# Two batches of a conditioned residual kernel as one product during its weight-loading phase, with base and rank terms put into PSUM banks

## The chip, the cores and the metric

One core of one Trainium2 chip runs the whole program. The metric is the device time of one execution in microseconds (us), the median of several runs. TensorE (PE in the profile) multiplies matrices, VectorE (DVE) and ScalarE (ACT) do elementwise work, GpSimd (POOL) and SyncE (SP) here mostly issue DMAs; ScalarE issues the stores of the output. SBUF holds tiles of 128 partitions[...].

## What is computed

For 8 batches b, with x[b] of 1024 x 512, cond[b] of 512, and weights:

```python
ae = layernorm(cond, ln_g, ln_b)
h  = gelu(ae @ w1 + b1)
xw = h @ w2 + b2                      # 8 x 8192
x_a, x_b = split(xw), each reshaped to (8, 512, 8)
layer = base + einsum('bdr,bkr->bdk', x_a, x_b)
x = x + (x + x @ layer)               # L0, its own residual and the outer one
ys = cond / sqrt(512)
d  = rsqrt((ys*ys) @ (weight*weight) + 1e-8)
x = x + ((x * ys) @ weight) * d       # L1
```

Both layers are linear in x, so the kernel makes one 512 x 512 matrix P[b] per batch and computes out[b] = x[b] @ P[b]:

- n[b] = I + diag(ys[b]) weight diag(d[b]), the matrix of L1 with its residual;
- P[b] = (2 I + base + x_a x_b^T) n[b] = (2 I + base) n[b] + x_a (n[b]^T x_b)^T. The first part is called q[b], the second is the rank term (rank 8).

f32 accuracy comes from splitting every operand into a high part in the format fp32r and the rest, and from three matmuls (high x high, high x rest, rest x high) for one.

## The kernel before

**Order.** `mm` (line 45) pins the order of all matmuls. Until `InOrder.on = False` (line 805) the instructions of VectorE, ScalarE and SyncE stand in the order of the source, too (`InOrder`, line 62 is the line that they all carry in the profile). After that, until the last two batches, a scheduler of the framework places those of VectorE, ScalarE and the DMAs, and lists in `after` (`at`, line 957) say behind which tile of the main part each step is emitted. Buffers are handed out by pools: a tile waits until whoever held its memory is through. `big` has nine buffers of 1 MB for weights, x, q and others; `acc` has four PSUM banks for products, `misc` and `xps` two each during the fill, replaced by `po` (four) in the main part.

**Fill.** While 16 groups of w2 (1 MB each, `w2_group`, line 389; each asks for its load on SyncE's queue at the place where its four matmuls stand) come in, TensorE makes q[0] to q[3], each alone: q[0] with `first_base`, the others with the class `Fill`, whose `units` (line 534) each do 3 matmuls: 4 chunks of the contraction by 4 row blocks by 3, 48 a batch. `n_half` makes two of four chunks of n[b] with VectorE, `round_right` makes its high part (ScalarE) and the rest (VectorE). The left matrix 2 I + base^T lies in `bh`/`bl`, split from `b_raw`, where the transposed base was loaded. Its four sums for the two-batch product (`left_sum`, line 368) are made at the very end of the fill.

**Rank term.** `rank_t` makes the right factor t, `with_bias`/`split`/`stack` the left factor a. `stack` brings them into rows of 4 batches (group g = 0 for batches 0 to 3, 1 for 4 to 7), keeps them in SBUF (`st_t`, `st_a`, pool `sp`), and stores them in DRAM (`kept_t`, `kept_a`). `load_rank(b)` (line 505) fetches 8 pieces of 64 KB for batch b on GpSimd's queue into the tiles `fa`, `ft` of `npool`; `rank_term(b)` (line 514) multiplies them into four `acc` banks and adds these to q[b] with VectorE. For batch 0 this is done straight from SBUF (`rank_first`, line 497, with the masked tile of `mask_t`), and base, loaded a second time untransposed (`b_nat`), is added to q[0] with 2 I on its diagonal. `split_p` splits P into `ph` (ScalarE) and `pl` (VectorE).

**Main part.** 48 tiles (batches 0 to 5, 8 tiles of 128 rows each): `main(b, t)` does 12 matmuls into a `po` bank, ScalarE copies it to `o` and issues its store. `load_x` and `split_x` prepare x four tiles ahead. Behind tiles stand `load_rank` 1 (tile 0), 2 (0), 3 (2), `rank_term` 1, 2, 3 (tiles 2, 5, 8), and from tile 11 on the class `Pair`, which makes q of two batches from seven products (Strassen's scheme) of 12 matmuls, for batches 4, 5 and 6, 7. `Pair.unit` (line 611) does half a product, 6 matmuls. Batches 6 and 7 are multiplied by seven products, too (`Seven`), at the end.

Of the kernel before, what the change touches and what calls it, by code (L numbers as in the profile page):

```python
# [30 lines left out]
def cond_resid_kernel(ctx: ExitStack, tc: tile.TileContext, small, cond, condrows, consts,  # L31
# [100 lines left out]
    def right_tiles(name):  # L132

        h = npool.tile([P, 2, D], F32R, tag="nh", name=f"nh_{name}")
        l = npool.tile([P, 2, D], F32R, tag="nl", name=f"nl_{name}")
        return h, l
# [196 lines left out]
    def n_half(b, j):  # L333

        n = npool.tile([P, 2, D], F32, tag="n", name=f"n_{b}_{j}", bufs=4)
        for kk in range(2):
            k = 2 * j + kk
            ve.scalar_tensor_tensor(n[:, kk, :], w_sb[:, k, :], ysT[:, k, b:b + 1],
                                           d_all[b], ALU.mult, ALU.mult)
            blk = n[:, kk, k * P:(k + 1) * P]  # L340
            ve.tensor_add(blk, blk, ident)
# [26 lines left out]
    def left_sum(i):  # L368
# [20 lines left out]
    def w2_group():  # L389
# [8 lines left out]
        if len(todo) == 6:  # L398
# [36 lines left out]
    def rank_t():  # L435
# [111 lines left out]
    class Pair:  # L547
# [63 lines left out]
        def unit(self):  # L611
# [55 lines left out]
    def split_x(b, j, part=None):  # L667
# [5 lines left out]
        if part != 0:  # L673
            ve.tensor_sub(xs[b, j][:, 1], t, xs[b, j][:, 0].bitcast(F32))
# [20 lines left out]
    class Fill:  # L695


        def __init__(self):
            self.bases = [Base(b) for b in (1, 2, 3)]
            self.ns, self.rests = {}, {}  # L700

        def units(self, count):
            for _ in range(count):
                if self.bases[0].at == 4 * KC:
                    self.bases.pop(0)
                self.bases[0].units(1)

        def make_n(self, b, j):
# [383 lines left out]
```

## Time and profile before

| | |
|---|---|
| median of 3 runs | 302.5 us (301.93 to 302.55) |
| the profiled execution | 302.08 us, its span 300.3 us |
| TensorE's clock | 1.00 over the span |
| first tile of the main part starts | 80.52 us |
| end of the main part's tiles | 254.59 us |
| DMA | 62.14 MB, mean 207 GB/s; 410 to 425 GB/s from 10 to 50 us |

Times within the execution are us from the start of the span. In the chain of waits a row is start, duration, what, and how many instructions; in the timeline of an engine start, duration, engine, line, operation, tiles out<-in, count and in brackets the idle time before it with what ended it; in the table of windows the stretch, its length, busy time (and count) of PE, PEld, DVE, ACT and POOL, the granted clock, the DMA share and GB/s; in the groups busy time and mean ns, then idle time before them. A tile's name has no buffer numbers: `w<-in_w` are the groups of w2 (and w1 where its tile is `w_sb`).

### The profile page before, as it was taken

Reading aid. Unit: us, or ns where it says so; the run is one execution under the profiler, and the core shown is the slowest. Engines: PE = TensorE matmul, PEld = TensorE weight load, DVE = VectorE, ACT = ScalarE, POOL = GpSimd, SP = SyncE. Lnnn points to the kernel's source line nnn. Section 1 sums busy time; section 2 is a strip of 40 time slices with the busy share of each in tenths; the row PEclk is TensorE's granted clock in tenths of the full one; section 3 lists DMA queues with packets and bytes.
Section 4 is the critical chain, followed back from the end, with each engine's and each line's share of the span. In section 5 each row is a group of like instructions: output and inputs, shape, how many; then the busy total and the mean of one; then the engine's idle time right before and its main releaser. Section 6 shows DMA issues by size and latency. Waiting matters only on the chain.

```text
span 300.3 us, 4005 instructions
## 1 busy us (share of the span) xinstructions
PE 293.4 (98%) x1501; PEld 227.1 (76%) x1501; DVE 211.0 (70%) x312; ACT 154.1 (51%) x226; POOL 34.8 (12%) x74
## 2 busy tenths in 40 slices
PE   7999999999999999999999999999999999999995
PEld 2655465466877778888887888888778888998995
DVE  4779840979569999935869994366562996479722
ACT  4757132256566673647634463656442663663630
POOL 0011000057004551000003600000000000000000
PEclk9999999999999999999999999999999999999999
DMA  7999999696619984605513841524516785131234
GB/s 210 410 428 419 405 424 419 219 326 183 197 70 305 306 288 126 239 35 210 204 43 97 230 164 46 201 55 192 210 70 210 244 267 227 38 140 49 93 140 142
DMA packets 19524, 62.14 MB, mean 207 GB/s; under 512 B 2720, under 2 KB 4000, under 8 KB 15152
## 3 DMA queue, kind: packets, MB, share of 16 engines
q1 hardware_dynamic: 6896, 39.57, 35.7%
q10 hardware_dynamic: 8832, 15.99, 14.2%
q0 software_dynamic: 3776, 6.31, 8.0%
q8 instruction: 12, 0.20, 0.3%
q14 instruction: 8, 0.07, 0.1%
HBM read 44.02 MB, written 17.84 MB: 206 GB/s over the span
## 4 chain that ended last, share of the span: by engine, by line
PE 84%; DVE 9%; ACT 3%; DMA 2%; issue 1%; SPq 0%; ACTq 0%
PE po L45 44%; PE pp L45 13%; PE pq L45 10%; PE sw L45 5%; PE px L45 4%; PE sz L45 2%; PE pg L45 2%; DVE n L62 2%; DMA b_raw<-in_baseT 2%; DVE sraw L62 1%; PE pr L45 1%; PE sv L45 1%; ACT o L62 1%; DVE sl L62 1%; ACT sh L62 1%
## 5 line engine op out<-in xcount | busy, mean ns | idle before, releaser
L45 PE MATMUL po<-ph,xs 128*128 128x512 f32 x384 | 123.8, 392 | 0.0
L45 PEld LDWEIGHTS po<-ph,xs 128*128 128x128 f32 x384 | 72.1, 188 | 16.8 <-issue 1.7
L45 PE MATMUL po<-pl,xs 128*128 128x512 f32 x192 | 74.8, 389 | 0.0
L62 ACT COPY o<-po 128x512 f32<-128x512 f32 x48 | 28.1, 586 | 52.8 <-PE po L45 52.8
L45 PEld LDWEIGHTS po<-pl,xs 128*128 128x128 f32 x192 | 36.1, 188 | 7.4
L62 DVE TENSOR_TENSOR xs<-x,xs 128x1024 fp32r<-128x1024 f32 x24 | 29.0, 1221 | 10.5 <-ACT xs L62 10.4
L62 ACT CAST xs<-x 128x1024 fp32r<-128x1024 f32 x24 | 24.9, 1052 | 3.7 <-DMA x<-in_x 1.9
L62 DVE TENSOR_TENSOR nl_p<-n,nh_p 128x1024 fp32r<-128x1024 f32 x14 | 17.1, 1222 | 12.3 <-ACT nh_p L62 12.2
L62 DVE TENSOR_TENSOR pl<-q,ph 128x1024 fp32r<-128x1024 f32 (+1 forms) x16 | 18.3, 1153 | 6.2 <-ACT ph L62 6.1
L62 DVE TENSOR_TENSOR q<-pr,q 128x512 f32<-128x512 f32 x32 | 20.1, 682 | 3.5 <-PE pr L45 3.5
L511 POOL DMA_DIRECT2D fa<-kept_a x28 | 13.7, 502 | 64.9 <-PE pr L45 64.8
L45 PE MATMUL pq<-nh,bh 128*128 128x512 f32 x48 | 19.8, 412 | 0.0
L45 PE MATMUL pq<-nl,bh 128*128 128x512 f32 x48 | 19.1, 398 | 0.1
L45 PE MATMUL pq<-nh,bl 128*128 128x512 f32 x48 | 19.0, 395 | 0.0
L62 DVE SCALAR_TENSOR_TENSOR n<-w_sb,ysT,d 128x512 f32<-128x512 f32 x24 | 17.7, 745 | 1.2 <-DMA d<-d_out 1.2
L62 ACT CAST nh_p<-n 128x1024 fp32r<-128x1024 f32 x14 | 14.8, 1054 | 6.3 <-PE pp L45 5.5
L62 ACT COPY o<-sw 128x512 f32<-128x512 f32 (+1 forms) x15 | 7.5, 500 | 19.2 <-PE sw L45 14.4
L62 ACT CAST ph<-q 128x1024 fp32r<-128x1024 f32 (+1 forms) x16 | 15.8, 1001 | 1.2 <-DVE q L62 0.8
L45 PE MATMUL px<-w,hT 128*32 128x512 f32 x128 | 16.0, 601 | 0.0
L62 ACT COPY q<-pp 128x512 f32<-128x512 f32 x20 | 11.7, 587 | 7.7 <-PE pp L45 7.7
L45 PEld LDWEIGHTS pq<-nh,bh 128*128 128x128 f32 x48 | 9.0, 188 | 8.4 <-issue 5.0
L511 POOL DMA_DIRECT2D ft<-kept_t x28 | 13.8, 509 | 5.2 <-DMA kept_t<-st_t 5.0
(185 smaller groups left out, 515.1 us busy)
## 6 DMA issues: line engine op xcount, KB each, us to landing
w<-in_w SPq DMA_DIRECT2D x16, 1024.0 KB, 10.5
x<-in_x SPq DMA_DIRECT2D x16, 1024.0 KB, 5.4
out<-o ACTq DMA_DIRECT2D x48, 256.0 KB, 3.2
out<-o ACTq DMA_DIRECT2D x6, 512.0 KB, 2.9
ft<-kept_t POOLq DMA_DIRECT2D x28, 64.0 KB, 3.4
fa<-kept_a POOLq DMA_DIRECT2D x28, 64.0 KB, 2.9
d<-d_out POOLq DMA_DIRECT2D x6, 256.0 KB, 5.2
w_sb<-in_weight SPq DMA_DIRECT2D x2, 512.0 KB, 5.3
```

Of the source, the lines that this page charges most:

```text
L45: tc.keep_in_program_order(nc.tensor.matmul(*args, **kw))
L62: return lambda *a, **kw: pin(f(*a, **kw)) if InOrder.on else f(*a, **kw)
L511: nc.gpsimd.dma_start(fold[name, b][32 * c:32 * c + 32, :], kept[name, g][32 * i:32 * i + 32, :])
```

## The change

- Batches 2 and 3 are made in the fill by `Pair(2)` instead of two bases; its last product (4) runs behind tiles 1 and 2 of the main part. The left sums are made in the middle of the fill (`left_raw`, `left_rest`). The four additions that end products 3 and 7 are held back (`hold`).
- `b_nat` is loaded two groups later. 2 I goes onto q[0]; `seed_first` puts q[0] + base into PSUM banks (`px` and `misc`), and the rank matmuls of batch 0 add onto them (32 rows, no mask). For batches 1 and 2, ScalarE copies q into the `acc` banks (`seed`), and the rank matmuls add onto that. `take` makes `ph` and `pl` of batches 0 to 2 out of the banks. Batch 3 stays as it was.
- The stacks of batches 4 to 7 are copied to `rows` and finished at the end of the fill (`late_rows`).
- `fa`, `ft` come from a new pool `folds`, opened after the fill's pools (`sp` among them) are closed. Loads and terms now: 1 (tiles 0, 3), 3 (1, 6), 2 (4, 9).
- The rest of the fourth x split of batch 0 is made by ScalarE (times -1) and an accumulating DMA; x (0, 1) is loaded in the fill. The identity is added to both blocks of a half of n in one instruction.

The diff, without the row of steps of the fill:

```diff
@@ -337,8 +337,8 @@
             k = 2 * j + kk
             ve.scalar_tensor_tensor(n[:, kk, :], w_sb[:, k, :], ysT[:, k, b:b + 1],
                                            d_all[b], ALU.mult, ALU.mult)
-            blk = n[:, kk, k * P:(k + 1) * P]
-            ve.tensor_add(blk, blk, ident)
+        blk = n.rearrange("p k (c i) -> p (k c) i", i=P)[:, 2 * j:2 * j + 6:5, :]
+        ve.tensor_add(blk, blk, ident.unsqueeze(1).to_broadcast([P, 2, P]))
         return n
     def round_right(n, name, wide=True):
@@ -365,7 +365,7 @@
     a11, a21 = b_raw[:, 0:2, 0:HD], b_raw[:, 0:2, HD:D]
     a12, a22 = b_raw[:, 2:4, 0:HD], b_raw[:, 2:4, HD:D]
-    def left_sum(i):
+    def left_raw(i):
         if i == 5:
             sraw["s"] = big_tile("sraw").rearrange("p k (u i) -> p k u i", u=2)
         s1, s2, s3, s4 = (sraw["s"][:, u] for u in range(4))
@@ -373,12 +373,14 @@
                        3: (s4, a12, s2, ve.tensor_sub), 7: (s3, a11, a21, ve.tensor_sub)}[i]
         op(s, x, y)
         h = cp.tile([P, 2, HD], F32R, name=f"sh_{i}")
+        se.copy(h, s)
+        sraw[i] = s, h
+    def left_rest(i):
+        s, h = sraw[i]
         l = cp.tile([P, 2, HD], F32R, name=f"sl_{i}")
-        se.copy(h, s)
         ve.tensor_sub(l, s, h.bitcast(F32))
         left[i] = h, l
-    b_nat = []
     px = [xps.tile([P, D], F32, name=f"px_{h}") for h in range(2)]
@@ -395,7 +397,7 @@
         if len(todo) == 8:
             sy.dma_start(crow, condrows)
             sy.dma_start(b2r, b2rows)
-        if len(todo) == 6:
+        if len(todo) == 4:
             b_nat.append(big_tile("b_nat"))
             sy.dma_start(b_nat[0], base)
         for j in range(4):
@@ -413,17 +415,27 @@
         ve.scalar_tensor_tensor(s, hi.bitcast(F32), neg_u, src, ALU.mult, ALU.add)
         return s
-    kept = {}
-    def stack(srcs, neg, name, g):
+    kept, late_rows = {}, []
+    def stack(srcs, neg, name, g, keep=None):
+        hi = None
         ps = misc.tile([P, D], F32, tag="misc", name=f"ps_{name}{g}")
         for i, src in enumerate(srcs):
             mm(ps, sel[:, g, :], src, start=(i == 0), stop=(i == len(srcs) - 1))
-        hi = work_tile()
-        se.copy(hi, ps)
+        if keep is None:
+            hi = work_tile()
+            se.copy(hi, ps)
+        else:
+            se.copy(keep, ps)
+            ps = keep
         def rest():
+            nonlocal hi
+            if keep is not None:
+                hi = work_tile()
+                se.copy(hi, ps)
             s = sp.tile([P, D], F32R, name=f"st_{name}{g}")
             ve.scalar_tensor_tensor(s, hi.bitcast(F32), neg, ps, ALU.mult, ALU.add)
             kept[name, g] = dram.tile([P, D], F32R, name=f"kept_{name}{g}")
@@ -463,24 +475,27 @@
         yield
         ve.tensor_sub(tl, t, th.bitcast(F32))
         yield
-        for g in range(2):
-            done = stack((th, tl), neg_t, "t", g)
-            yield
-            stt[g] = done()
-            yield
+        done = stack((th, tl), neg_t, "t", 0)
+        yield
+        stt[0] = done()
+        yield
+        late_rows.append(stack((th, tl), neg_t, "t", 1, rows[:, 3, :]))
+        yield
     def times_d(b, c):
         ve.tensor_mul(q[b][:, c, :], q[b][:, c, :], d_all[b])
-    def twice_i_plus_base():
-        for c in range(KC):
-            blk = b_nat[0][:, c, c * P:(c + 1) * P]
-            ve.scalar_tensor_tensor(blk, ident, 2.0, blk, ALU.mult, ALU.add)
-    def add_base(b):
-        for c in range(KC):
-            ve.tensor_add(q[b][:, c, :], q[b][:, c, :], b_nat[0][:, c, :])
+    b_nat = []
+    def twice_i_first():
+        blk = q[0].rearrange("p k (c i) -> p (k c) i", i=P)[:, 0:16:5, :]
+        ve.scalar_tensor_tensor(blk, ident.unsqueeze(1).to_broadcast([P, KC, P]), 2.0, blk,
+                                ALU.mult, ALU.add)
+    def seed_first(c, ps):
+        ve.tensor_add(ps, q[0][:, c, :], b_nat[0][:, c, :])
     def round_w(k):
         se.copy(wh[:, k, :], w_sb[:, k, :])
@@ -488,38 +503,53 @@
     def rest_w(k):
         ve.tensor_sub(wl[:, k, :], w_sb[:, k, :], wh[:, k, :].bitcast(F32))
-    tm = {}
-    def mask_t():
-        tm[0] = sp.tile([P, D], F32R, name="tm_0")
-        ve.tensor_scalar_mul(tm[0], stt[0].bitcast(F32), mask[:, 0:1])
-    def rank_first(c):
-        ps = misc.tile([P, D], F32, tag="misc", name=f"pr_0_{c}")
-        mm(ps, sa[0][:, c * P:(c + 1) * P], tm[0], start=True, stop=True)
-        ve.tensor_add(q[0][:, c, :], ps, q[0][:, c, :])
-    fold = {}
+    def seed(b, c, ps):
+        se.copy(ps, q[b][:, c, :])
+    def take(b, c, ps):
+        se.copy(ph[b][:, c, :], ps)
+        ve.tensor_sub(pl[b][:, c, :], ps, ph[b][:, c, :].bitcast(F32))
+    def onto(ps, a, t):
+        mm(ps, a, t, start=False, stop=True, skip_group_check=True)
+    def rank_first(c, ps):
+        onto(ps, sa[0][0:32, c * P:(c + 1) * P], stt[0][0:32, :])
+    fold, pools = {}, {}
     def load_rank(b):
         for name in ("a", "t"):
             g, i = divmod(b, 4)
-            fold[name, b] = npool.tile([P, D], F32R, tag=f"f{name}", name=f"f{name}_{b}", bufs=2)
+            fold[name, b] = pools["fold"].tile([P, D], F32R, tag=f"f{name}", name=f"f{name}_{b}", bufs=2)
             for c in range(KC):
                 nc.gpsimd.dma_start(fold[name, b][32 * c:32 * c + 32, :],
                                     kept[name, g][32 * i:32 * i + 32, :])
-    def rank_term(b):
+    def rank_term(b, take_p=False):
         ps = [acc.tile([P, D], F32, tag="acc", name=f"pr_{b}_{c}") for c in range(KC)]
+        if take_p:
+            for c in range(KC):
+                seed(b, c, ps[c])
         for c in range(KC):
             at = slice(32 * c, 32 * c + 32)
-            mm(ps[c], fold["a", b][at, c * P:(c + 1) * P], fold["t", b][at, :],
-               start=True, stop=True)
+            a, t = fold["a", b][at, c * P:(c + 1) * P], fold["t", b][at, :]
+            if take_p:
+                onto(ps[c], a, t)
+            else:
+                mm(ps[c], a, t, start=True, stop=True)
         for c in range(KC):
-            ve.tensor_add(q[b][:, c, :], ps[c], q[b][:, c, :])
+            if take_p:
+                take(b, c, ps[c])
+            else:
+                ve.tensor_add(q[b][:, c, :], ps[c], q[b][:, c, :])
     class Base:
@@ -628,11 +659,16 @@
                 se.copy(c21, bank)
             elif p == 6:
                 se.copy(c12, bank)
+            elif p == 3 and hold is not None:
+                hold.append(lambda: ve.tensor_add(c12, bank, c12))
             elif p == 3:
                 ve.tensor_add(c12, bank, c12)
             elif p == 7:
                 se.copy(c22, bank)
-                ve.tensor_add(c22, c22, c21)
+                if hold is not None:
+                    hold.append(lambda: ve.tensor_add(c22, c22, c21))
+                else:
+                    ve.tensor_add(c22, c22, c21)
             elif p == 2:
                 ve.tensor_add(c11, bank, c11)
             else:
@@ -671,7 +707,19 @@
             xs[b, j] = big.tile([P, 2, KC, 2 * P], F32R, tag="big", name=f"xs_{b}_{j}")
             se.copy(xs[b, j][:, 0], t)
         if part != 0:
-            ve.tensor_sub(xs[b, j][:, 1], t, xs[b, j][:, 0].bitcast(F32))
+            hi, lo = xs[b, j][:, 0], xs[b, j][:, 1]
+            if b == 0 and j > 2:
+                se.mul(lo, hi.bitcast(F32), -1.0)
+                nc.gpsimd.dma_start(lo, x[b, j // 2][:, :, (j % 2) * 2 * P:(j % 2 + 1) * 2 * P],
+                                    accum_op=ALU.add)
+            else:
+                ve.tensor_sub(lo, t, hi.bitcast(F32))
+    def split_first(m):
+        hi, lo = xs[0, 0][:, 0], xs[0, 0][:, 1]
+        at = slice(m * P, (m + 1) * P)
+        ve.tensor_sub(lo[:, :, at], raw[0, 0][:, :, at], hi[:, :, at].bitcast(F32))
     stt, sa = [None, None], [None, None]
@@ -962,12 +1022,13 @@
     pairs = {}
     place = lambda i: divmod(i, NTT)
-    for b in range(1, 4):
-        first = (b - 1) * NTT
-        at(*place(max(0, 3 * b - 7)), load_rank, b)
-        at(*place(3 * b - 1), rank_term, b)
-        for j in range(2):
-            at(*place(first + 3 + j), split_p, b, j)
+    at(*place(1), two.unit)
+    at(*place(2), two.unit)
+    for b, load, spot in ((1, 0, 3), (3, 1, 6), (2, 4, 9)):
+        at(*place(load), load_rank, b)
+        at(*place(spot), rank_term, b, b < 3)
+    for j in range(2):
+        at(*place(19 + j), split_p, 3, j)
     for b, spots in ((4, [11 + 3 * n // 4 for n in range(14)]), (6, [24 + 2 * n // 3 for n in range(14)])):
         first, end = spots[0], spots[-1] + 1
@@ -1006,7 +1067,7 @@
         if t == 0 and i + NTT < TILES:
             p_tiles(b + 1)
         main(b, t)
-        if t % 4 == 0 and i + 4 < TILES:
+        if t % 4 == 0 and 0 < i < TILES - 4:
             load_x(*divmod(i // 4 + 1, NHALF))
         if t % 2 == 0 and i + 4 < TILES:
             split_x(*divmod(i // 2 + 2, NTT // 2))
```

The steps of the fill after the change, from where `fill.make_n(2, 0)` stood (before it, batch 1 is as it was):

```python
two = Pair(2)
two.make_n(1)
w2_group()
w2_group()
base1.units(4)
two.round(1)
two.make_n(2)
two.round(2)
left_raw(5)
two.finish(1)
left_raw(6)
left_rest(5)
left_raw(7)
left_raw(3)
left_rest(6)
twice_i_first()
w2_group()
w2_group()
base1.units(6)
w2_group()
steps = rank_t()
next(steps)
left_rest(7)
w2_group()
next(steps)
base1.units(2)
left_rest(3)
two.finish(2)
two.unit()
two.make_n(5)
w2_group()
next(steps)
two.round(5)
two.finish(5)
w2_group()
two.unit()
next(steps)
two.unit()
next(steps)
two.unit()
two.make_n(6)
w2_group()
next(steps)
two.round(6)
next(steps)
w2_group()
bank = [px[1], misc.tile([P, D], F32, tag="misc", name="pr_0_1")]
p_tiles(0)
for c in range(2):
    seed_first(c, bank[c])
two.unit()
two.finish(6)
two.round(3)
next(steps)
w2_group()
w2_group()
two.unit()
two.round(7)
w2_group()
load_x(0, 0)
load_x(0, 1)
bias = with_bias(0)
bank.append(px[0])
hi = work_tile()
se.copy(hi, bias)
seed_first(2, bank[2])
s = work_tile()
ve.scalar_tensor_tensor(s, hi.bitcast(F32), neg_u, bias, ALU.mult, ALU.add)
xa = (s,)
two.finish(3)
two.units(2)
done = stack(xa, neg_a, "a", 0)
two.finish(7)
sa[0] = done()
held = []
bank.append(misc.tile([P, D], F32, tag="misc", name="pr_0_3"))
seed_first(3, bank[3])
two.unit(held)
two.unit(held)
for c in range(KC):
    rank_first(c, bank[c])
split_x(0, 0, 0)
split_first(0)
for c in range(KC):
    take(0, c, bank[c])
two.unit(held)
two.unit(held)
late_rows.append(stack(xa, neg_a, "a", 1, rows[:, 0, :]))
split_first(1)
split_x(0, 1)
two.round(4)
two.finish(4)
for f in held:
    f()
for i in range(2):
    f = late_rows[i]()
    (stt if i == 0 else sa)[1] = f
InOrder.on = False
setup.close()
po = ctx.enter_context(tc.tile_pool(name="po", bufs=4, space=PSUM))
pools["fold"] = making.enter_context(tc.tile_pool(name="folds", bufs=2))
pools["o"] = making.enter_context(tc.tile_pool(name="opool", bufs=4))
```

More of the change, by code (lines that the diff above doesn't have):

```diff
@@ L132, in right_tiles @@
     def right_tiles(name):
-        h = npool.tile([P, 2, D], F32R, tag="nh", name=f"nh_{name}")
-        l = npool.tile([P, 2, D], F32R, tag="nl", name=f"nl_{name}")
+        h = npool.tile([P, 2, D], F32R, tag="nh", name=f"nh_{name}", bufs=3)
+        l = npool.tile([P, 2, D], F32R, tag="nl", name=f"nl_{name}", bufs=3)
         return h, l
@@ L609, in product, with unit @@
                        stop=(kk == 1 and i == 2), skip_group_check=not first)
-        def unit(self):
+        def unit(self, hold=None):
             p, s = self.todo.pop(0)
@@ L693, in cond_resid_kernel, with round1 @@
     first_base(3, (1, 2, 3))
[L695 to L708, printed above, removed]
-            self.ns[b, j] = n_half(b, j)
-        def round(self, b, j):
-            self.rests[b, j] = round_right(self.ns[b, j], f"{b}_{j}", b == 3)
-        def finish(self, b, j):
-            next(f for f in self.bases if f.b == b).add(self.rests[b, j]())
-    fill = Fill()
-    fill.make_n(1, 0)
-    fill.round(1, 0)
-    fill.make_n(1, 1)
+    base1, n1 = Base(1), {}
+    def round1(j):
+        n1[j] = round_right(n1[j], f"1_{j}", False)
+    n1[0] = n_half(1, 0)
+    round1(0)
+    n1[1] = n_half(1, 1)
     keep_first((0, 1))
-    fill.round(1, 1)
+    round1(1)
     keep_first((2, 3))
-    fill.finish(1, 0)
+    base1.add(n1[0]())
     for c in range(2):
         times_d(0, c)
-    fill.finish(1, 1)
+    base1.add(n1[1]())
     for c in range(2, KC):
@@ L733, in cond_resid_kernel @@
         round_w(k)
-    fill.units(4)
+    base1.units(4)
     for k in range(2, KC):
         rest_w(k)
-    fill.make_n(2, 0)
+    two = Pair(2)
+    two.make_n(1)
     w2_group()
     w2_group()
-    fill.units(4)
-    fill.round(2, 0)
-    fill.make_n(2, 1)
-    fill.finish(2, 0)
+    base1.units(4)
+    two.round(1)
[9 more added lines that the diff above has]
+    twice_i_first()
     w2_group()
     w2_group()
-    fill.units(6)
+    base1.units(6)
     w2_group()
@@ L749, in cond_resid_kernel @@
     next(steps)
+    left_rest(7)
     w2_group()
     next(steps)
-    fill.units(4)
+    base1.units(2)
[3 more added lines that the diff above has]
+    two.make_n(5)
     w2_group()
     next(steps)
+    two.round(5)
+    two.finish(5)
     w2_group()
-    fill.units(2)
-    fill.round(2, 1)
+    two.unit()
     next(steps)
-    fill.finish(2, 1)
+    two.unit()
     next(steps)
-    fill.units(3)
-    twice_i_plus_base()
+    two.unit()
+    two.make_n(6)
     w2_group()
     next(steps)
+    two.round(6)
+    next(steps)
     w2_group()
-    next(steps)
-    mask_t()
-    add_base(0)
-    fill.units(2)
-    fill.make_n(3, 0)
+    bank = [px[1], misc.tile([P, D], F32, tag="misc", name="pr_0_1")]
+    p_tiles(0)
+    for c in range(2):
+        seed_first(c, bank[c])
+    two.unit()
+    two.finish(6)
+    two.round(3)
     next(steps)
@@ L773, in cond_resid_kernel @@
     w2_group()
-    next(steps)
-    fill.units(2)
+    two.unit()
+    two.round(7)
     w2_group()
     load_x(0, 0)
-    xa = (split(with_bias(0)),)
-    fill.round(3, 0)
-    fill.units(4)
+    load_x(0, 1)
+    bias = with_bias(0)
+    bank.append(px[0])
+    hi = work_tile()
+    se.copy(hi, bias)
[5 more added lines that the diff above has]
+    two.units(2)
     done = stack(xa, neg_a, "a", 0)
-    fill.finish(3, 0)
+    two.finish(7)
     sa[0] = done()
-    fill.units(3)
-    fill.make_n(3, 1)
-    p_tiles(0)
-    rank_first(0)
-    rank_first(1)
-    fill.round(3, 1)
-    fill.units(2)
-    split_p(0, 0, 0)
-    rank_first(2)
-    rank_first(3)
-    split_p(0, 0, 1)
-    fill.finish(3, 1)
-    split_p(0, 1)
-    split_x(0, 0)
-    fill.units(4)
-    sa[1] = stack(xa, neg_a, "a", 1)()
-    left_sum(5)
-    fill.units(8)
-    split_x(0, 1)
-    for p in (6, 3, 7):
-        left_sum(p)
+    held = []
[3 more added lines that the diff above has]
+    two.unit(held)
+    for c in range(KC):
+        rank_first(c, bank[c])
+    split_x(0, 0, 0)
+    split_first(0)
+    for c in range(KC):
+        take(0, c, bank[c])
[3 more added lines that the diff above has]
+    split_first(1)
+    split_x(0, 1)
+    two.round(4)
+    two.finish(4)
+    for f in held:
+        f()
+    for i in range(2):
+        f = late_rows[i]()
+        (stt if i == 0 else sa)[1] = f
     InOrder.on = False
@@ L808, in cond_resid_kernel @@
     po = ctx.enter_context(tc.tile_pool(name="po", bufs=4, space=PSUM))
-    pools = {"o": making.enter_context(tc.tile_pool(name="opool", bufs=4))}
+    pools["fold"] = making.enter_context(tc.tile_pool(name="folds", bufs=2))
+    pools["o"] = making.enter_context(tc.tile_pool(name="opool", bufs=4))
     def main(b, t):
```

## The prediction

> **What bounds the kernel now.** I read the page first, then the chain of waits, the stages by window, and the timelines of the two DMA-issuing queues.
>
> ```profile
> PE 293.4 (98%) x1501; PEld 227.1 (76%) x1501; DVE 211.0 (70%) x312; ACT 154.1 (51%) x226; POOL 34.8 (12%) x74
> ```
>
> The page says TensorE, but a matmul's record is longer than its share of a dense stream, so "98%" proves nothing alone. The chain does:
>
> ```profile
> 74.85 5.67 PE pq L45 x24
> 80.52 8.19 PE po L45 x36
> 88.70 0.44 PE pr L45 x2
> 89.14 8.39 PE po L45 x36
> ```
>
> 24 matmuls in 5.67 us is 0.236 us each, 36 in 8.19 is 0.2275. From 80.52 to 254.6 the chain is TensorE alone, without a pause: the fill ends at 80.52 when the first `po` starts, and everything that delays TensorE in the main part delays the end by as much. In the fill itself the starts of the matmuls leave only some 0.3 us open (at 71.3) after 27.3. The second resource there is the DMA:
>
> ```profile
> 30.00:40.00 10.00, 10.00 (x59) 5.67 (x59) 7.75 (x15) 1.98 (x4) 0.00 (x0) 1.00 1.01 410
> 40.00:50.00 10.00, 10.00 (x60) 5.16 (x59) 2.14 (x3) 3.85 (x7) 0.00 (x0) 1.00 1.01 421
> ```
>
> The last two columns are DMA share and GB/s: full up to 50 us. 1 MB takes 1.049 MB / 0.42 MB per us = 2.5 us in this stream, so w2 has no slack to lose. When its groups are asked for:
>
> ```profile
> 31.17 1.19 SPq L62 DMA_DIRECT2D w<-in_w  x2
> 36.02 0.33 SPq L62 DMA_DIRECT2D b_nat<-in_base  x1
> 36.87 20.46 SPq L62 DMA_DIRECT2D w<-in_w  x6
> ```
>
> And the rank term's way through DRAM, on GpSimd's queue:
>
> ```profile
> 78.07 0.57 POOL L430 DMA_DIRECT2D kept_a<-st_a  x1 [2.84 <-DVE st_a L62]
> 89.53 1.95 POOL L511 DMA_DIRECT2D fa<-kept_a  x4 [10.89 <-PE pr L45]
> 91.47 1.95 POOL L511 DMA_DIRECT2D ft<-kept_t  x4
> ```
>
> and, of `fa` and `kept_a` together, the view of the tile:
>
> ```profile
> DMA to landing us min/median/max: 2.0/2.9/6.1
> ```
>
> Eight small loads take 3.9 us to issue (0.49 each) and 2.0 to 6.1 to land. Today those of batches 1 and 2 are issued by 75 us, before the main part, and nothing waits for them.
>
> [...] `pq` matmuls that were ready stood behind `pr` at 71.3. [...] `fa` and `ft` loads rose to 6 us and more beside two 1 MB loads of x at 90 to 101. [...]
>
> **The change, part by part.** The rows used:
>
> ```profile
> L62 DVE TENSOR_TENSOR xs<-x,xs 128x1024 fp32r<-128x1024 f32 x24 | 29.0, 1221 | 10.5 <-ACT xs L62 10.4
> L62 DVE TENSOR_TENSOR q<-pr,q 128x512 f32<-128x512 f32 x32 | 20.1, 682 | 3.5 <-PE pr L45 3.5
> L62 ACT COPY q<-pp 128x512 f32<-128x512 f32 x20 | 11.7, 587 | 7.7 <-PE pp L45 7.7
> ```
>
> Back to back, these come every 1.14, 0.64 and 0.54 us.
>
> *TensorE.* Batches 2 and 3 cost 96 matmuls, as a pair 7 x 12 = 84: 12 x 0.235 = -2.8 us. Product 4 (12 matmuls, 2.75 us) moves behind tiles 1 and 2 of the main part: that is a move, not a saving. Before the last w2 group 3 matmuls more are done (+0.7), after it fewer.
>
> *w2's queue.* The built order shows that SP's load of the tenth w2 group (w2 0,0,1) now goes into `b_raw`'s buffer and waits for the fourth left sum; behind it stand two w2 loads, and behind `sl_3` stand `base` and the rest. VectorE is free for batch 2 when `d_2` lands, 32.7 to 33.8 (33.84 in the trace, with a w2 load beside it that now comes later). Then two halves of n at 1.87 (0.67+0.75+0.45), four half-wide sums, `nl` of product 1 (1.14) and `sl_5`: 3.75 + 4.4 = 8.1 us, so the load goes out at 40.8 to 41.9 instead of 32.0. A lone 1 MB load takes 4.9 us (5.4 median for x): landing 46.3, the next at 48.8. TensorE wants them at 46.0 and 47.6: +1.25 (0.6 to 2.2). The last w2 group, issued when group 12 is consumed, stands behind a later queue and d_4's 0.5 MB: +0.4 (0 to 0.9). It is consumed at 63.5+0.7+1.65 = 65.85, called X.
>
> *From X to the main part* (65.85 for 63.48 before). VectorE adds the bias (X+0.7), base into a bank (1.4), splits (2.2), then `nl_p3`, `nl_p7` (4.45); `st_a` at 5.1, the last seed at 5.7. TensorE does products 6 and 3 to X+6.0, the rank matmuls to 6.95, product 7 to 9.75. ScalarE copies four P tiles to 8.65, VectorE's four subtractions end at 9.4: both under product 7. But the first `po` also waits for ScalarE's copy of the late row, behind the two copies of product 7: 10.6+0.5 = 11.1. So TensorE idles 1.15 us and the main part begins at X+11.2 = 77.05, called T; 80.52 before: -3.45.
>
> *After T.* ScalarE's queue holds three splits of x and the new multiply by -1 ahead of `nh` of product 4: 0.96 x 3 + 1.15 + 1.05, ready at T+5.1, `nl` at 6.4. Two tiles cover 5.46, the first matmul 0.2: +0.7 stall. The accumulating DMA is not in the trace: [...] it is harmless up to some 14 us, since its tile is read after T+24; I take 5.
>
> *The fold loads, the largest cost.* The new `folds` pool takes over the memory of `sp`, where `st_t` and `st_a` lie, so the first `fa` load waits until the late stores have landed, and the seven others stand behind it in GpSimd's queue. VectorE's queue after T: split of x (1.1 to 2.3), n sum, split, wait for `nh` (5.15), `nl` (6.4), four q_3 additions (8.9), two row splits: `st_a` at T+10.3. The store of `kept_a` landed 2.3 and 3.8 us after its issue: T+13.3. Eight issues to 16.8, the last landing 2.2 to 4 later, since x_1_1 (issued about T+12.6) shares the engines: T+19.0. TensorE arrives at T + 4 x 2.73 + 2 x 1.37 + 0.7 = 14.4: stall 4.6 us (3.5 to 7). Behind these rank matmuls stands every later `po`. Cover today: the loads are issued before the main part; that cover is gone.
>
> *At nothing.* Seeds by ScalarE (4 x 0.54 a batch) stand ready before their matmuls, in the 14 us after T and before tile 9. VectorE saves about 2.6 us a batch in P (four additions dropped); it is not the bound once the fold has stalled TensorE. Merged identity adds save 0.15 each, counted above. The tail keeps its order and shifts: 0, +-0.3.
>
> *Sum.* -3.45 (start of the main part, with the fill's 2.8 saving, the moved product, and +0.7, +1.65, +1.15 in it) + 2.75 (product 4) + 0.7 + 4.6 = +4.6. Span 300.3 + 4.6 = 304.9; the profiled execution is 1.8 longer than its span, so 306.7 against 302.1. The runs' median is 0.4 above that execution: **307.0**.
>
> **Rivals.** (A) As summed, 304.5 to 309. (B) *Faster*: the stores and fold loads land under tiles 0 to 3. From 307.0 take 4.6: 302.4; with w2 in time (-1.65) 300.8. It decides if `st_a` is done by T+5 rather than T+10.3: 1 store (2.9) + 3.4 + 2.5 would end at 13.8. For it: VectorE has less to do in all. Against it: the row splits stand behind `nl` of product 4 and four additions, in order. (C) *The fill's loads become the bound*: `d_2` lands late, w2 groups follow one another with DRAM stores and d_4 among them; X slips 2 to 3 us more: 309 to 311. For it: a full DMA share until 50. Against: only 5 us of DMA time are lost, and groups after the third had 1 to 4 us of lead. (D) The fold stall is half hidden (2 to 3 us), 302.9 to 304.5, if store and loads all take their minimum and `nh` of product 4 comes sooner.
>
> **Chances.** A 0.58, C 0.17, D 0.14, B 0.07, other 0.04. Some 0.2% (0.6 us) is what a measurement of this kernel can tell from no change. Faster by more 0.07, within 0.03, slower 0.90. The range 303.0 to 310.5 leaves out B and the far end of C.
>
> **What would show it.** Right: the wait list has `pr` after the fourth `po` waiting 3.5 to 7 us for DMA `fa` or `ft`; w2's tenth load issued near 41; first `po` at 76 to 78; a pause of about 1 us before it. Wrong: `pr` does not wait (B); first `po` past 79 (C); a pause elsewhere in the main part, where I found only cover.

## The result, and the profile after

The changed kernel takes **313.49 us** (median of 6 runs, 311.31 to 314.39) against 302.5 (6 runs, 301.93 to 302.55): a ratio of 1.036 (95% interval 1.033 to 1.039), slower. The profiled execution took 313.51 us, its span is 311.7: 11.4 more than the 300.3 of before. Forecast were 307.0 and +4.6.

The page of the kernel after, engines and granted clock over the 40 slices:

```profile
PE 295.4 (95%) x1489; PEld 227.0 (73%) x1489; DVE 212.6 (68%) x299; ACT 163.9 (53%) x246; POOL 36.0 (12%) x75
PEclk9999999999996699999999999999999999999999
```

Twelve matmuls fewer than before, as planned, yet TensorE is busy 2.0 us longer: some of its matmuls are slower. The second line says when: in the two slices from 93.5 to 109 us the clock is at 0.6 of full speed. Before it was 1.00 over the whole span. What TensorE waited for (total us, times, longest):

```profile
PE pr L45 <- DMA ft<-kept_t: 5.8, 1, 5.8
PE px L45 <- DMA w<-in_w: 3.0, 4, 0.8
PE po L45 <- ACT rows L62: 0.9, 1, 0.9
```

The chain of waits of the kernel after (start, duration, what):

```profile
41.22 8.52 DMA w<-in_w
...
66.49 1.07 PE px L45 x8
...
78.90 2.86 ACT xs L62 x3
...
84.96 1.11 DVE q L62 x2
...
87.36 0.75 DVE st_t L62
...
89.06 2.56 DMA kept_a<-st_a
92.32 1.97 POOL fa L531 x4
95.24 3.97 DMA ft<-kept_t
99.22 2.06 PE pr L45 x4
101.28 10.86 PE po L45 x36
112.58 8.43 PE po L45 x36
```

From 80.52 to 254.6 the chain of before was TensorE alone. Now it leaves TensorE at 77.80, ahead of the main part. It runs through ScalarE's splits of x and VectorE's additions for q[3] and `st_t`, then through the store of `kept_a`, the issue of the loads and the landing of `ft`, and comes back at 99.22. Then look at the two rows of 36 `po` matmuls: 10.86 us for the first, 8.43 for the second, the same work. The windows show the same twice over, the fill's DMA and the clock (length, busy time of PE, PEld, DVE, ACT, POOL, clock, DMA share, GB/s):

```profile
30.00:40.00 10.00, 10.00 (x59) 5.78 (x52) 9.28 (x15) 3.24 (x4) 0.00 (x0) 1.00 0.94 343
40.00:50.00 10.00, 7.80 (x48) 3.60 (x50) 9.38 (x14) 5.39 (x10) 0.00 (x0) 1.00 0.87 332
...
100.00:110.00 10.00, 10.00 (x31) 7.61 (x31) 2.48 (x4) 3.18 (x6) 5.18 (x11) 0.67 0.45 119
```

In the first two, 410 and 421 GB/s have become 343 and 332, and VectorE has become the nearly full engine (9.28 and 9.38 us of 10). In the third, 10 us hold 31 matmuls at a clock of 0.67. At full speed one starts every 0.2275 us (36 in 8.19 us before, where the record of one lasts 392 ns), which makes 44. After the pause the matmuls start 0.43 us apart, until 106.5.

The queues that set the two places, first SyncE's with w2, then GpSimd's with the rank term (start, duration, out<-in, count, idle before and what ended it):

```profile
32.21 10.04 SPq L62 DMA_DIRECT2D w<-in_w  x4
```

```profile
89.06 0.53 POOL L442 DMA_DIRECT2D kept_a<-st_a  x1
92.32 1.97 POOL L531 DMA_DIRECT2D fa<-kept_a  x4 [2.73 <-DMA kept_a<-st_a]
94.28 1.94 POOL L531 DMA_DIRECT2D ft<-kept_t  x4
```

The tenth w2 load, the second of the four in the first row, went out at 40.80 (32.03 before). The first fold load waited 2.73 us for the store of `kept_a` to land; before, the loads of batches 1 and 2 were issued ahead of the main part.

**Where the 11.4 us went.** Each term is read from the trace at the place where the prediction put it. The four `pr` matmuls of batch 1 each read their own pieces of `fa` and `ft`, so the pause has two parts, up to the first of them and up to the last:

| term | forecast | measured |
|---|---|---|
| first `po` (80.52 before) | -3.45 (77.05) | -1.57 (78.95) |
| product 4 in the main part | +2.75 | +2.75 |
| stall ahead of product 4 | +0.7 | +0.3 |
| pause up to the last piece: ahead of the first `pr` | +4.6 | +5.8 |
| the same: from the first `pr` to the last | in the 4.6 | +1.3 |
| slow matmuls after that | not in the sum | +2.8 |
| sum | +4.6 | +11.4 |

The last two: four `pr` and 36 `po` matmuls took 2.06 + 10.86 = 12.92 us; the rows of `pr` and of 36 `po` matmuls behind it that were shown of before took 0.44 + 8.39 = 8.83. The difference of 4.1 us is not all slow matmuls. Before, the four `pr` started together, at 88.64. Now they start at 99.22, 99.65, 100.13 and 100.52, each 0.09 to 0.14 us after its piece of `ft` landed (99.08, 99.52, 100.04, 100.43). So 1.3 us of it is still waiting for the loads, and 2.8 us is the low clock.

The first row takes 80.52 from the chain, as the prediction did. That is where the chain's row begins; the first `po` itself started at 80.35. From start to start the gain is 1.40 us, and the terms then exceed the 11.4 us by 0.15.

### The profile page after: what moved, and what is told of

It is laid out like the page before. It is cut to its first block, busy times and chain, and to the rows that moved or that the text cites. A ratio compares the mean times of both kernels' runs of the same rounds, so it can differ in the third digit from the quotient of the medians.

```text
span 311.7 us, 3995 instructions
## 1 busy us (share of the span) xinstructions
PE 295.4 (95%) x1489; PEld 227.0 (73%) x1489; DVE 212.6 (68%) x299; ACT 163.9 (53%) x246; POOL 36.0 (12%) x75
## 4 chain that ended last, share of the span: by engine, by line
PE 78%; DMA 9%; DVE 5%; ACT 4%; issue 2%; POOL 1%; SPq 0%; ACTq 0%; POOLq 0%; DVEq 0%
PE po L45 40%; PE pp L45 17%; PE sw L45 6%; DMA w<-in_w 5%; PE sz L45 3%; PE px L45 3%; PE pg L45 3%; PE pq L45 2%; PE pr L45 2%; DMA b_raw<-in_baseT 2%; PE sv L45 1%; DMA ft<-kept_t 1%; ACT xs L62 1%; DVE sraw L62 1%; DMA kept_a<-st_a 1%
## 5 line engine op out<-in xcount | busy, mean ns | idle before, releaser
L62 DVE TENSOR_TENSOR xs<-x,xs 128x1024 fp32r<-128x1024 f32 (+1 forms) x24 | 27.8, 1175 | 15.3 <-ACT xs L62 15.2
L62 DVE TENSOR_TENSOR nl_p<-n,nh_p 128x1024 fp32r<-128x1024 f32 x21 | 25.6, 1221 | 15.0 <-ACT nh_p L62 15.0
L62 ACT CAST nh_p<-n 128x1024 fp32r<-128x1024 f32 x21 | 22.1, 1052 | 11.1 <-DVE n L62 9.4
L62 ACT COPY q<-pp 128x512 f32<-128x512 f32 x30 | 17.6, 587 | 17.3 <-PE pp L45 17.3
L62 DVE TENSOR_TENSOR q<-pr,q 128x512 f32<-128x512 f32 x20 | 12.5, 681 | 13.0 <-PE pr L45 13.0
L45 PE MATMUL pp<-nh_p,sh 128*128 128x512 f32 x48 | 19.1, 399 | 0.0
L45 PE MATMUL pp<-nl_p,sh 128*128 128x512 f32 x48 | 18.8, 393 | 0.0
L45 PE MATMUL pp<-nh_p,sl 128*128 128x512 f32 x48 | 18.7, 390 | 0.0
L62 DVE TENSOR_TENSOR n<-n,n 128x1024 f32<-128x1024 f32 x12 | 14.6, 1219 | 0.2
L45 PE MATMUL pp<-nl_p,bh 128*128 128x512 f32 x36 | 14.3, 397 | 0.2 <-DVE nl_p L62 0.2
L45 PE MATMUL pp<-nh_p,bh 128*128 128x512 f32 x36 | 14.4, 400 | 0.0
## 6 DMA issues: line engine op xcount, KB each, us to landing
w<-in_w SPq DMA_DIRECT2D x16, 1024.0 KB, 10.3
```

Of the source, the lines that this page charges most:

```text
L45: tc.keep_in_program_order(nc.tensor.matmul(*args, **kw))
L62: return lambda *a, **kw: pin(f(*a, **kw)) if InOrder.on else f(*a, **kw)
```

## The experiments

Two theories stood against each other after this reading. **Theory**: three separate losses, that of the fill's loads, that of the rank term's way through DRAM, and a TensorE that runs slowly for some us after it has stood still; the third is a consequence of the second. **Rival**: the waits are tied to each other (a full VectorE, a full DMA), so that one that is taken away comes back elsewhere, and the slow matmuls belong to what runs there and not to the pause. Measured beside these runs, the kernel before took 302.19 to 302.35 us.

**e1: the late rows first**, ahead of all other late work of VectorE.

```diff
     late_rows.append(stack(xa, neg_a, "a", 1, rows[:, 0, :]))
+    for i in range(2):
+        f = late_rows[i]()
+        (stt if i == 0 else sa)[1] = f
     split_first(1)
...
     for f in held:
         f()
-    for i in range(2):
-        f = late_rows[i]()
-        (stt if i == 0 else sa)[1] = f
```

> Edit: the two late row sets (t and a of batches 4 to 7) are finished and stored right after their last copy, before the rest of x's first tile and product 4, not after them; everything else as in the changed kernel. Theory (the fold loads of batch 1 stand behind these stores, the rank matmuls wait for them, and the pause also lowers TensorE's granted clock): st_a is ready at about 81 instead of 88, the loads land before the fourth tile ends, the 5.8 us wait of pr goes, the clock stays at 1.00; product 4 waits about 1.3 us more. 313.5 - 5.8 - 4.1 + 1.3 = 304.9 (303.5 to 306). Rival (the w2 groups that come late in the fill are the loss): no change of more than 1 us, since the fill is the same. Rival (DRAM loads beside x_1_1 are slow whenever they are issued): the wait shrinks by less than half, 309 to 312.

308.83 us, ratio 1.019 (1.014 to 1.023): better than after, 4 us short of what was expected. `pr` no longer waits. The waits of TensorE, and GpSimd's queue in this kernel, show what took its place:

```profile
PE po L45 <- DMA xs<-in_x: 3.0, 1, 3.0
```

```profile
93.61 1.32 POOL L713 DMA_DIRECT2D xs<-in_x  x1
```

The accumulating DMA of the fourth x split, which had been issued at 83.15 and had landed at 88.73 in the kernel after, now stands behind 16 fold loads in the queue. It landed at 104.88, 11.3 us after its issue, and tile 6 needs it. Its gap of 3.35 us is again followed by matmuls 0.43 us apart. This profiled execution was the slowest of four (311.42 us): in the two fastest, 306.85 and 308.01 us, the mean clock was 0.998 and 1.000, where a single stretch of 3.41 us at half speed, as in e11 and e7 below, would by its length lower the mean by 0.006 (e7's mean is 0.994), so they had no such stretch.

**e2: the rank terms later**, everything else as after.

```diff
-    for b, load, spot in ((1, 0, 3), (3, 1, 6), (2, 4, 9)):
+    for b, load, spot in ((1, 0, 6), (3, 1, 8), (2, 4, 10)):
```

> Edit: the rank terms of batches 1, 3, 2 are placed behind tiles 6, 8, 10 instead of 3, 6, 9; loads and stores as in the changed kernel. Theory: TensorE has three tiles (8.2 us) more before it needs the folds, more than the 5.8 us wait: no pause, no lower clock, 313.5 - 9.9 = 303.6 (302.5 to 305), unless P of batch 1, due at tile 8, now comes late (up to +2). Rival (the clock falls for another reason than the pause, the load on the chip in the early main part): the two slices at 0.66 stay, 307 to 308. Rival (fill): no change of more than 1 us.

304.35 us, ratio 1.007 (1.005 to 1.009): as expected. One line of numbers takes away 9.1 of the 11.0 us. The clock stays at full speed over the whole span, and of the wait only this is left:

```profile
PE pr L45 <- DMA ft<-kept_t: 1.1, 1, 1.1
```

**e3: the left sums ahead of the n of product 1**, so that the tenth w2 load can go out sooner: `left_raw` of 5, 6, 7, 3 moved to stand before `two.make_n(1)`.

> Edit: the four left sums (raw and high part) are made ahead of n of batch 2, so that the buffer of the transposed base is free earlier for the tenth w2 group. Theory: that load goes out near 34 to 36 instead of 40.8, the four waits of px for w2 (3.0 us) shrink to 0.8 or less; the pause before pr and the lower clock stay: 313.5 - 2.4 = 311.1 (310 to 312.5). Rival (the fill's loads are the main loss and push the fold loads, too): 308 or less. Rival (DMA is simply full in the fill): less than 0.8 us gained.

314.18 us, ratio 1.039 (1.037 to 1.041): missed, no gain. With the sums earlier in the program, the buffer of the transposed base, which the fourth sum is the last to read, was handed to the *eighth* w2 load, no longer to the tenth. The eighth and ninth went out at 35.0 and 36.4 instead of 30.8 and 32.2. One wait of 2.4 us stands where four shorter ones had been, and its gap of 2.95 us brings slow matmuls into the fill, too.

**e4 and e5: the pause filled.** Matmuls that keep TensorE busy stand ahead of `pr` of batch 1, 20 in e4, 30 in e5.

```diff
     def rank_term(b, take_p=False):
...
+        if b == 1:
+            idle = po.tile([P, D], F32, tag="po", name="idle")
+            for _ in range(20):
+                mm(idle, xs[0, 0][:, 0, 0, 0:P], ph[0][:, 0, :], start=True, stop=True)
```

> Edit: 20 extra matmuls (128x512, result not used, 4.6 us) behind the fourth tile, ahead of the rank matmuls of batch 1, so that TensorE works through most of the wait. The work added lies inside the wait. Theory (the pause itself lowers the granted clock): the wait that is left is 1 to 2 us, the matmuls after it run at 0.228 us instead of 0.43, 313.5 - 4.1 = 309.4 (308.5 to 310.5). Rival (the clock falls for another reason): the slices at 0.66 stay and the time too, 313 to 314.5.

315.27 us, ratio 1.042 (1.040 to 1.045): missed. `pr` still waited 2.5 us, since the fold loads landed later this time (the last at 102.09, not 100.43), and the gap of 2.92 us was followed by slow matmuls until 107.7.

> The kernel after, with 30 matmuls (their result is not used) ahead of pr of batch 1 instead of 20: they fill the pause of 5.8 us nearly whole. Theory (a pause of about 3 us or more halves TensorE's clock for 6 to 7 us, and that is 4.1 us of the loss): the largest gap between two matmul starts there is under 2 us, the clock stays full, the matmuls after it come every 0.228 us; 313.5 - 4.1 = 309.4 us (308.5 to 310.3). Rival (the slow matmuls come from the eight loads or from the tiles that follow, not from the pause): still slow matmuls after it, 313 us or more.

313.94 us, ratio 1.038 (1.035 to 1.042): missed as well. The gap is down to 1.03 us, but after it came a shorter slow stretch, 103.1 to 106.5. The granted clock of this kernel:

```profile
PEclk9999999999999799999999999999999999999999
```

In one of e5's four executions (312.40 us) the mean clock was 1.000. So these two don't settle what the slow clock is worth. The wait is for memory, and a filled wait is no shorter. In e5 the third fold load needed 6.5 us beside a load of x, and `pr` began at 100.48.

**e6: the left sums between the two**, after the rounding of product 1 and ahead of the n of product 2.

> The kernel after, with the four left sums right behind the rounding of product 1's n, ahead of the n of product 2. Their buffer is taken at the same place among the w2 groups as in the kernel after. Theory (the tenth w2 load waits for VectorE's fourth sum): that load goes out about 2.4 us sooner, near 38.4, and the waits of px fall from 3.0 to about 0.8: 311.3 us (310.5 to 312.3), with pr's pause and the low clock as they were. Rival (the loads of the fill are bound by the DMA engines' throughput anyway): waits of px stay near 3.0, 313 to 314 us.

317.94 us, ratio 1.051 (1.048 to 1.053): missed, and the worst of all. The sums' own buffer is asked for at the same place, but that of the transposed base again goes to the eighth w2 load, and its last reader comes later than in e3: the load went out at 38.74. Two waits, 6.2 us together, and slow matmuls. e3 and e6 say the same: the wait belongs to the buffers, and moving the work that frees them only moves the wait to another load.

**e7: e1 without the accumulating DMA**, VectorE subtracting as for the other x splits (the condition `b == 0 and j > 2` is never met).

> As e1 (late rows finished first), and the rest of the fourth x split by one subtraction of VectorE instead of ScalarE's multiply and the accumulating DMA. Theory (what e1 kept of the loss is the 3.0 us wait for that DMA, queued behind the fold loads, and the low clock after that gap): both go, 308.8 - 3.0 - 1.6 = 304.2 us (303.2 to 305.3), no gap over 1.5 us in the main part. Rival (the wait moves again, to VectorE or to product 4): 306 us or more, with a new wait of over 1.5 us.

307.94 us, ratio 1.018 (1.017 to 1.020), not to be told from e1: the rival was right. The DMA's wait is gone, and product 4 waits instead:

```profile
PE pp L45 <- DVE nl_p L62: 1.3, 1, 1.3
PE pp L45 <- ACT nh_p L62: 0.8, 1, 0.8
```

The rows' work and the subtractions of x stand ahead of `nh` and `nl` of product 4, on ScalarE and on VectorE. Gaps of 1.15 and 1.75 us, one matmul between them, were followed by 3 us of slow matmuls.

**e8: e2, e6 and the plain subtraction together.**

> Three edits together: rank terms behind tiles 6, 8, 10, left sums behind the first rounding, plain subtraction for the fourth x split. Theory (the losses of the kernel after are pr's pause with the clock, and the fill's late loads, and they add): from the 304.35 of e2, 1.1 for the rest of pr's wait at most and 2.0 for the fill's waits: 301.5 us (300.8 to 302.6), at or a little below the kernel before. Rival (the waits are tied to others that come forward when they go): 303.5 us or more.

308.08 us, ratio 1.020 (1.017 to 1.022): missed, for the reason of e6: `px` waits 4.5 us, the main part starts at 82.80. `pr` doesn't wait at all.

**e9: the left sums out of the 1 MB buffers.**

```diff
-            sraw["s"] = big_tile("sraw").rearrange("p k (u i) -> p k u i", u=2)
+            sraw["s"] = ppool.tile([P, KC, D], F32, tag="pl", name="sraw").rearrange(
+                "p k (u i) -> p k u i", u=2)
...
+    left_rest(7)
+    left_rest(3)
+    work = ppool.tile([P, KC, D], F32R, tag="pl", name="work2")
     steps = rank_t()
     next(steps)
-    left_rest(7)
...
-    left_rest(3)
```

> The kernel after, with the four raw left sums in a tile of the pool of P (free at that time) instead of one of the nine 1 MB buffers; the rest of sums 7 and 3 is made ahead of the rank steps, because that memory is wanted next by them. Theory (the fill's loads are late because two of the nine buffers, that of the transposed base and that of the sums, are held until about 41 us, and moving the sums only hands the wait to an earlier load): the tenth load now waits for TensorE alone and goes out sooner, the waits of px fall from 3.0 to about 1.0, no gap over 2 us in the fill: 311.5 us (310.5 to 312.7); pr's pause and the low clock stay. Rival (it is the place of the sums on VectorE, not the buffers): waits of px near 3.0, 313 us or more.

312.14 us, ratio 1.031 (1.028 to 1.034): within what was expected. SyncE's queue and the longest wait of this kernel:

```profile
30.92 12.33 SPq L62 DMA_DIRECT2D w<-in_w  x4
```

```profile
PE pr L45 <- DMA fa<-kept_a: 6.7, 1, 6.7
```

The waits of `px` are gone, no gap in the fill is longer than 1.62 us, and the main part starts at 77.61. That is 1.34 earlier than after, and nearly the 77.05 of the forecast. But `pr` starts only 0.5 earlier: its pause has grown by 0.9 of what the fill gained.

**e10: every loss taken out.** e9, the spots of e2, the plain subtraction, product 4 behind tiles 2 and 3, and the late row's product one half product earlier.

> Every loss found taken out of the kernel after: sums as in e9; rank terms behind tiles 6, 8, 10; plain subtraction for the fourth x split; product 4 behind tiles 2 and 3; the late row's product one half product earlier, so that the first tile doesn't wait for its copy. Theory (the losses are separate and add): from the 304.35 of e2 take 1.1 (pr), 2.0 (px), 0.9 (row copy), 0.2 (product 4): 300.2 us (299.3 to 301.5), faster than the kernel before. Rival (each wait that goes brings another forward, as in the earlier runs): 302 us or more, with a wait of over 1 us at a new place.

301.99 us, ratio 0.999 (0.998 to 1.000): missed by 1.8 us, equal to the kernel before. `pr` and the row copy don't wait, and the clock is full. Two waits come from its own edits:

```profile
PE po L45 <- ACT o L62: 1.2, 1, 1.2
PE ps_t L45 <- DVE st_t L62: 0.7, 1, 0.7
```

The first: on ScalarE the copies of two output tiles stood behind the copy of product 4's second half, for which TensorE was not there yet (ScalarE idle for 2.01 us, until 90.00), and the four `po` banks (tiles of 128x512 f32 in PSUM, into which this kernel's matmuls write) were full.

**e11 and e12: one pause in the kernel before.** These measure the disputed cost alone, in the middle of the main part, with nothing of the change in the kernel.

```diff
         nc.scalar.dma_start(out[b, t * P:(t + 1) * P, :], o)
+        if (b, t) == (2, 4):
+            z = [cp.tile([P, 64], F32R, name=f"z_{i}") for i in range(2)]
+            nc.gpsimd.dma_start(z[0], o[:, 0:64].bitcast(F32R))
+            nc.gpsimd.dma_start(z[1], z[0])
+            idle = po.tile([P, D], F32, tag="po", name="idle")
+            mm(idle[0:64, :], z[1], ph[b][:, 0, :], start=True, stop=True)
```

(e11: one `z`, one DMA.)

> The kernel BEFORE, with one matmul more behind tile 20 of the main part that reads 64 columns of the output tile just made, brought by one small DMA (its result is not used): TensorE stands still once, for the copy, the DMA's issue and its landing, about 3.2 us. Theory (a standstill of about 3 us is followed by a stretch of matmuls at half speed): a stretch of 0.43 us matmuls of 3 to 4 us follows, so the time is 302.35 + 3.2 + 1.6 = 307.2 us (306.3 to 308.5). Rival (the slow matmuls of the kernel after belong to its loads and rank matmuls, not to the standstill): none follow, 302.35 + 3.2 = 305.6 us or less.

307.99 us, ratio 1.018 (1.015 to 1.021). The stretch after the pause, as windows and in the chain:

```profile
160.00:165.00 5.00, 4.79 (x14) 3.85 (x15) 0.89 (x1) 0.74 (x2) 0.00 (x0) 0.66 0.00 0
165.00:170.00 5.00, 5.00 (x24) 3.67 (x23) 3.02 (x4) 1.97 (x3) 1.43 (x3) 1.00 0.14 52
```

> As e11 with two such DMAs one after the other: a standstill of about 5.5 us in the kernel BEFORE. Theory: a stretch of 0.43 us matmuls of 6 to 7 us follows, 302.35 + 5.5 + 3.3 = 311.2 us (310 to 312.5). Rival (no slow stretch): 302.35 + 5.5 = 307.9 us or less.

310.45 us, ratio 1.025 (1.021 to 1.028). Its wait, and its chain after it:

```profile
PE idle L45 <- DMA z<-z: 5.7, 1, 5.7
```

```profile
162.79 4.93 PE pp L45 x12
167.73 2.73 PE po L45 x12
```

Both confirm the theory. In e11 the gap is 4.07 us from start to start, 3.84 more than usual. The next six matmuls come at full speed, then eight every 0.43 us. 3.84 + 0.23 (the added matmul) + 8 x 0.2 = 5.7; the span grew by 5.6 (305.9). In e12 the 12 matmuls of the half products after the pause take 4.93 us instead of 2.75, and 5.81 + 0.23 + 12 or 13 x 0.2 = 8.5; the span grew by 8.7 (309.0). Nothing runs on the DMA engines in the first row of e11, which holds its slow stretch (share 0.00), so the loads aren't its cause.

**e13 and e14**: e10 with product 4 back behind tiles 1 and 2 (e14), and with `st_t` ahead of the rounding of product 6 as well (e13). First the expectation of e13, then that of e14:

> As e10, with product 4 back behind tiles 1 and 2, and st_t of the rank term made ahead of the rounding of product 6. Theory (two of the waits of e10, 1.2 us of po on ScalarE behind product 4's copy and 0.7 us of ps_t on VectorE, come from these two places alone): both go, product 4 waits 0.3: 302.0 - 1.6 = 300.4 us (299.8 to 301.3), faster than the kernel before. Rival (the waits come back elsewhere): 301.7 us or more.

> As e10, with product 4 back behind tiles 1 and 2 alone. Theory: the wait of po on ScalarE goes (1.2), product 4 waits 0.3, ps_t still waits 0.7: 301.1 us (300.5 to 301.8). Rival (product 4 then waits for VectorE as in the seventh and eighth run, 0.8 to 2.1 us): 302 us or more.

e14: 302.54 us, ratio 1.001 (1.001 to 1.002). Missed: the wait of `po` went (1.2), but product 4 waits 1.7 and `ps_t` 1.2. The rival's mechanism. e13: **301.26 us, ratio 0.997 (0.996 to 0.998)**, 1.0 us faster than the kernel before beside it (302.29), at the upper end of what its theory gave. `ps_t` waits no more, but product 4 waits 1.7 us where the theory had 0.3, so in this point the rival was right:

```profile
PE pp L45 <- DVE nl_p L62: 1.7, 1, 1.7
```

Had product 4's `nl` been in time, the span of 299.5 would be some 297.8. That was not tried.

## Why the prediction was wrong

The direction and the place of the largest loss were right; the time, 313.49 us, lies above the range of 303.0 to 310.5. By its own steps:

- **The sum, "-3.45 + 2.75 + 0.7 + 4.6 = +4.6", lacked a term: what a pause does to TensorE afterwards.** This is the step that failed. The prediction priced a stall at its length and put nothing for the matmuls behind it, without a reason. In the trace they cost 2.8 us more. e11 and e12 show the cost alone, in the kernel before: pauses of 3.8 and 5.8 us are followed by 8 and by 12 or 13 matmuls at half speed, 1.5 and 2.7 us of the spans' growth. The trace of before has no such case: from 25 to 262 us the longest gap between two starts in it is 0.61 us, at a clock of 1.00. The traces of the slow stretches give the pitch, 0.43 us at a clock of 0.50, and the lengths: 3.41 us (e11), 6.83 (e12, its mean clock 0.989 over 309.0 us) and 10.24 (the kernel after, from 96.32 to 106.56). The shortest gaps before them, leaving e5 and e7 aside, were 2.92 us (e4) and 2.95 us (e3).
- **Two terms that were in the sum were too small.** Of the 6.8 us between +4.6 and +11.4, 2.8 are the missing term, 2.5 the pause (7.1 instead of 4.6) and 1.9 the start of the main part; the stall of product 4 gives 0.4 back.
- *The pause*, forecast 4.6 (3.5 to 7): 5.8 up to the first `pr` and 7.1 up to the last, which is what the forecast reckoned to. The mechanism was right at every step: `st_a` done at T+9.8 (forecast T+10.3; VectorE's additions came every 0.60 us, not 0.64), `kept_a` landed at T+12.7 (T+13.3), the first `fa` load waited for it (2.73 us idle on GpSimd), the eighth was issued by T+17.3 (T+16.8). Only the last landing was too optimistic: T+21.5 instead of T+19.0. The forecast took 2.2 us for it, the low end of its own 2.2 to 4, and each of the eight took 4.3 to 4.8 us beside a load of x.
- *w2's queue*, forecast +1.25 and +0.4: four waits of 3.0 in all, for the ninth, tenth, eleventh and sixteenth group. The tenth load went out at 40.80, inside the forecast; it landed at 47.27 instead of 46.3. The wait for the *ninth* was overlooked: it went out at 32.21 and landed at 42.49, where before it had gone out at 31.17 and landed at 39.99. e9 shows that this was no property of the DMA engines but of two buffers: the waits vanish with one buffer more.
- *From X to T.* X, the end of the last group's matmuls, came at 67.56 (the chain's row at 66.49) instead of 65.85, and T 11.4 us after it instead of 11.2. Of the 1.7 us by which X came late, the waits of `px` explain 1.35; the rest is not traced to a place. The row copy's wait was forecast at 1.15 and is 0.9. The parts that the prediction names for its -3.45 (-2.8, -2.75, +0.7, +1.65, +1.15) make only -2.05.
- *Product 4*: 12 matmuls in the main part, as forecast; its stall was 0.3 instead of 0.7.
- *At nothing*: right. The accumulating DMA took 5.6 us and nobody waited; the 5 that were taken for it were the author's estimate, and the trace of before has no such DMA. e1 shows how thin that cover was: issued 10 us later, it cost 3.0 us and, in the profiled execution, the clock. The identity add over 128x256 took 422 ns (mean of 14), where before two of 128x128 took 288 each: 0.15 us saved, as reckoned. The seeds and `take` cost TensorE nothing. These groups replace part of the 32 additions of before, and VectorE waits for `pr`, not TensorE for it:

```profile
L62 DVE TENSOR_TENSOR q<-pr,q 128x512 f32<-128x512 f32 x20 | 12.5, 681 | 13.0 <-PE pr L45 13.0
L62 DVE TENSOR_TENSOR pl<-pr,ph 128x512 fp32r<-128x512 f32 x10 | 6.4, 682 | 1.0 <-ACT ph L62 1.0
```

- *The rivals.* (B), that the loads land in time, was excluded as forecast. (C) came nearest by its number (309 to 311), but is not what happened: X came 1.7 us late where (C) says 2 to 3. "`pr` waits 3.5 to 7" and "tenth load near 41" were found, "first `po` past 79" was just not (78.95), and no sign had been named for the clock.

Of the theory that the losses are separate, e2 is for it (one loss taken out, 9.1 of its 9.9 us gone, the clock's term with it). e1, e3, e6, e7 and e14 are against it as a rule: in each a wait that went came back at another place, on VectorE, in the queue of GpSimd or in the hand-out of buffers. What the change itself was worth is seen only with its losses taken out: e13 is 1.0 us faster than before, where 12 matmuls fewer are 2.8 us.

## What to carry to other kernels

Price a stall of TensorE twice: its length up to the last operand that lands, and the slow matmuls after it: in these runs they followed every gap of 2.92 us or more (for one of 3.01 us it can't be told), and in this kernel a pause of 7.1 us cost 9.9. Moving the rank terms one to three tiles later took nearly all of both away. When a tile is taken from a shared pool, ask which later load then waits for which buffer. Moving the work that frees the buffer moved the wait, and one buffer more removed it. When a wait is taken out by putting its work first in a queue, look at what stands behind it in that queue, its DMAs too.

## What was not expected of the hardware

- After every gap of 2.92 (e4) to 7.11 us (e9) between two starts matmuls of 512 columns came every 0.43 us instead of 0.2275. (For one gap of 3.01 us in e6, which has a second of 4.23 us soon after, it can't be told.) After most gaps of 1.0 to 2.2 us they did not (in the kernel after five of 1.09 to 1.33 us, at a clock of 1.00). Two cases stand out: 1.15 and 1.75 us close together in e7, and 1.03 us followed by four rank matmuls in e5, each followed by 3 to 3.4 us of slow ones.
- The granted clock in the traces fits these cases better than the length of a gap. It is 1.00 or 0.50, and within a run it changes only at whole multiples of 3.41 us from one another. Laid out in steps of that length (from 30 to 250 us, all 16 traces), 12 of the 13 falls come after a step in which TensorE stood still for 1.9 us or more, counting gaps over 0.6 us less 0.23 us for a matmul. The steps at full clock that no fall follows hold 2.0 us or less. In the kernel after the fall at 96.32 comes after a step with 3.1 us of standstill; its other steps at full clock hold 1.1 or less, and before has no gap over 0.6 us there. By this count it matters where a pause lies, and two short ones in one step add up (1.15 and 1.75 us in e7). Steps of e11, then of e7:

```profile
158.22:161.63 3.41, 1.42 (x6) 1.19 (x7) 2.67 (x4) 0.67 (x1) 0.02 (x1) 1.00 0.24 68
161.63:165.04 3.41, 3.41 (x10) 2.66 (x9) 0.00 (x0) 0.78 (x2) 0.00 (x0) 0.50 0.00 0
165.04:168.45 3.41, 3.41 (x17) 2.37 (x16) 1.47 (x2) 1.93 (x3) 0.00 (x0) 1.00 0.00 0
```

```profile
85.20:88.62 3.42, 1.79 (x7) 1.27 (x8) 3.42 (x5) 1.50 (x3) 3.28 (x8) 1.00 0.96 334
88.62:92.03 3.41, 3.41 (x10) 2.64 (x9) 2.74 (x4) 3.32 (x6) 3.00 (x7) 0.50 0.89 244
92.03:95.44 3.41, 3.41 (x16) 2.79 (x15) 0.67 (x1) 1.47 (x3) 0.75 (x2) 1.00 0.82 192
```

- So the slow stretch can begin late: in e11 2.0 us of the pause lie in the first of these steps, and the clock falls at its end, 1.4 us and six full-speed matmuls after the restart. In e7 the two pauses put 1.9 us into one step. The fall in e5 does not fit: its step, 99.57 to 102.98, holds 0.8 us of standstill, and then the four rank matmuls of 32 rows, one after another until 102.04. Whether such matmuls count for less is open, and no run was made to test this reading.
- The same accumulating DMA of 0.5 MB took 5.6 us in the kernel after and 11.3 us in e1, where fold loads and a load of x were under way.
